# Eleven dense products of a relational graph layer: eight block products against Strassen's seven

## The chip, the cores and the metric

The kernel runs on one core of one Trainium2 chip. The metric is the device time of one execution in microseconds (us), lower being better.

## The reference

The input is `x` (1250 rows of 1024 float32) and 20000 edges, each with a source row, a destination row (the edges are sorted by destination) and one of eight types. What is computed:

```python
h = relu(layernorm(x))                       # 1250 x 1024
u = h @ root + bias
for r in range(8):                           # edge types
    sums = segment_sum(h[src] * (type == r), dst)
    cnt  = segment_sum(type == r, dst)
    u += (sums / maximum(cnt, 1)) @ weight[r]
z = concat([u, h]) @ w_gate + b_gate         # w_gate is 2048 x 1024
out = x + tanh(u) * z + h * (1 - z)
```

So there are eleven dense products of 1250x1024 by 1024x1024: eight with `weight[r]`, one with `root`, and two with the halves of `w_gate`. All of them are float32.

## The kernel before, in words

The rows are cut into ten blocks of 128 (the last has 98). The kernel multiplies first and gathers afterwards: it computes `y[r] = h @ weight[r]` for all rows and writes it to DRAM, and an edge then adds one row of `y[type]`, scaled by 1/count, to its destination row.

**The products.** `transposed` (L102, L104) turns a row block into eight 128x128 blocks that are the stationary operand. `product` (L111) runs, for each of the eight pieces of the inner dimension and each half of the 1024 columns, one 128x128 by 128x512 matmul; in the trace each is two MATMUL instructions. The weights are loaded by `load_w` (L92) on SyncE's queue, one matrix ahead. `step(s, d)` does matrix `s` for block `d`: for the eight typed weights ScalarE copies the two PSUM banks out (L174) and writes `y` (L175), for `root` VectorE adds them to `u` (L179), for the lower half of `w_gate` it adds the bias and stores `z` (L183) over the transposed `h`, in the tile `hz`.

**The slots.** Beside the first two matrices, `slots(c0)` takes eight chunks of 128 edges at a time (`CG = 8`) and works out with one-hot comparisons on VectorE and small bf16 matmuls on TensorE the rank of every edge among those of its destination. An indirect DMA from GpSimd (L347) scatters each edge's row number into `table`. There are 26 slots for each destination for types 0 to 4, and 20 for types 5 to 7.

**The edges.** Slots are gathered in two groups: group 0 (types 0 to 4) beside matrices 5 to 7, group 1 (types 5 to 7) beside `root` and the lower half of `w_gate`. For each slot and row block, `add_slot` issues an indirect DMA on GpSimd that brings 128 rows of `y` into the tile `got` (L418; five buffers), and VectorE does `u = got * w + u` (L422). That makes 10 x 26 + 10 x 20 = 460 gathers. The ten blocks of `u` stay in the on-chip memory. A rare path for more slots stands between the groups under a condition and is not taken with these inputs.

**The end.** `finish(d)` transposes `u`, multiplies it by the upper half of `w_gate`, and works out the result on VectorE and GpSimd (L507 to L515).

The order of instructions on each engine is fixed ahead of the run by a planner: it goes through the program with its own durations and takes on each engine, among the instructions that are ready, the one that comes first in the program. A tile's buffer is handed on only when all who use it are done.

Of the kernel before, what the change touches and what calls it, by code (L numbers as in the profile page):

```python
# [18 lines left out]
def tile_rgcn_highway(  # L19
# [22 lines left out]

    nc = tc.nc
# [5 lines left out]
    NH = D // 512  # L49
    ND = -(-N // P)  # L50
    NCH = -(-E // P)
# [8 lines left out]
    CG = 8  # L60
# [9 lines left out]
    wpool = ctx.enter_context(tc.tile_pool(name="wpool", bufs=2 * KC))  # L70
    rows = ctx.enter_context(tc.tile_pool(name="rows", bufs=2))
# [3 lines left out]
    h_dram = dram.tile([N, D], F32, name="h_dram")  # L75
    keys_dram = dram.tile([NCH * P], I32, name="keys_dram")
# [5 lines left out]
    def ps_tr():  # L82
        return psum.tile([P, 4, P], F32, name="ps_tr", bufs=2)

    def ps_mm():
        return psum.tile([P, 512], F32, name="ps_mm", bufs=4)

    def load_w(w):
        tiles = []
        for k in range(KC):  # L90
            t = wpool.tile([P, D], F32, name="w_t")
            nc.sync.dma_start(t, w[k * P:(k + 1) * P, :])  # L92
            tiles.append(t)
        return tiles

    def transposed(to, of, n):

        for g in range(KC // 4):
            p = ps_tr()
            for i in range(4):  # L100
                k = 4 * g + i
                nc.tensor.transpose(p[:, i, :n], of[:n, k * P:(k + 1) * P], ident[:n, :n])  # L102
            copy = nc.vector.tensor_copy if g % 2 else nc.scalar.copy
            copy(to[:, 4 * g:4 * g + 4, :n], p[:, :, :n])  # L104

    def product(aT, n, w):

        banks = [ps_mm() for _ in range(NH)]
        for k in range(KC):
            for j in range(NH):  # L110
                nc.tensor.matmul(banks[j][:n], aT[:, k, :n], w[k][:, j * 512:(j + 1) * 512],  # L111
                                 start=(k == 0), stop=(k == KC - 1))
        return banks
# [5 lines left out]
    bias_bc = const.tile([P, D], F32, name="bias_bc")  # L119
    bgate_bc = const.tile([P, D], F32, name="bgate_bc")  # L120
# [4 lines left out]
    first = const.tile([P, NCH], F32, name="first")  # L125
    count = const.tile([P, R * ND], F32, name="count")
    drc = const.tile([P, R + G, ND], F32, name="drc")
    runs = const.tile([P, NHI], F32, name="runs")

    hz = [keep.tile([P, D], F32, name=f"hz{d}") for d in range(ND)]  # L130

    def hT(d):
        return hz[d].rearrange("p (k f) -> p k f", k=KC)


    w_t = None
    for d in range(ND):
        n = nrows(d)
        xt = rows.tile([P, D], F32, name="xt")
        nc.sync.dma_start(xt[:n], x[d * P:d * P + n, :])  # L140
        if d == 0:
            w_t = load_w(weight[0])
        st = rows.tile([P, NH, 6], F32, name="st")
        for j in range(NH):
            nc.vector.bn_stats(st[:n, j, :], xt[:n, j * 512:(j + 1) * 512])  # L145
        mv = rows.tile([P, 2], F32, name="mv")
        nc.vector.bn_aggr(mv[:n], st[:n].rearrange("p a b -> p (a b)"))
        sd = rows.tile([P, 1], F32, name="sd")
        nc.scalar.activation(sd[:n], mv[:n, 1:2], AF.Sqrt, bias=eps[:n])
        rs = rows.tile([P, 1], F32, name="rs")  # L150
        nc.vector.reciprocal(rs[:n], sd[:n])
        nc.vector.tensor_scalar(xt[:n], xt[:n], mv[:n, 0:1], 0.0, op0=OP.subtract, op1=OP.max)
        nc.scalar.activation(xt[:n], xt[:n], AF.Copy, scale=rs[:n])  # L153
        nc.sync.dma_start(h_dram[d * P:d * P + n, :], xt[:n])
        transposed(hT(d), xt, n)


    mats = [weight[r] for r in range(R)] + [root, w_gate[D:, :]]
    cur = {"w": w_t, "next": None}

    def step(s, d):

        n = nrows(d)
        if d == 0:
            if s:
                cur["w"] = cur["next"]
            cur["next"] = load_w(mats[s + 1] if s + 1 < len(mats) else w_gate[:D, :])
        banks = product(hT(d), n, cur["w"])
        if s < R:
            g = max(i for i in range(G) if R0[i] <= s)  # L170
            o = (s - R0[g]) * N + d * P
            t = rows.tile([P, D], F32, name="yt", bufs=3)
            for j, b in enumerate(banks):
                nc.scalar.copy(t[:n, j * 512:(j + 1) * 512], b[:n])  # L174
            nc.scalar.dma_start(y[g][o:o + n, :], t[:n])  # L175
        elif s == R:
            for j, b in enumerate(banks):
                c = slice(j * 512, (j + 1) * 512)
                nc.vector.tensor_add(u_acc[d][:n, c], u_acc[d][:n, c], b[:n])  # L179
        else:  # L180
            for j, b in enumerate(banks):
                c = slice(j * 512, (j + 1) * 512)
                nc.vector.tensor_add(hz[d][:n, c], b[:n], bgate_bc[:n, c])  # L183

    steps = iter([(s, d) for s in range(len(mats)) for d in range(ND)])


    with ExitStack() as early:
        ix1 = early.enter_context(tc.tile_pool(name="ix1", bufs=1))
        ix = early.enter_context(tc.tile_pool(name="ix", bufs=2))  # L190

        far = ix1.tile([P, sum(n_slots) // P], I32, name="far")
        nc.gpsimd.memset(far, FAR)
        nc.scalar.dma_start(table.rearrange("(p f) o -> p (f o)", p=P), far)


        C2 = NCH - P
        ed = {}
        for name, of, pad in (("dst", dst, 3 * KEYS), ("typ", etype, R), ("src", src, 0)):
            t = ix1.tile([P, 2, P], I32, name=f"e_{name}")  # L200
            nc.gpsimd.memset(t[:, 1, :], pad)
            nc.scalar.dma_start(t[:, 0, :], of[:P * P].rearrange("(c p) -> c p", p=P))
            nc.scalar.dma_start(t[:C2 - 1, 1, :],
                                of[P * P:(NCH - 1) * P].rearrange("(c p) -> c p", p=P))
            nc.scalar.dma_start(t[C2 - 1:C2, 1, :EL], of[None, (NCH - 1) * P:])
            ed[name] = t
        nc.scalar.dma_start(bias_bc, bias[None, :].to_broadcast([P, D]))
        nc.scalar.dma_start(bgate_bc, b_gate[None, :].to_broadcast([P, D]))

        f = {}  # L210
        for name in ("dst", "typ", "src"):
            f[name] = ix1.tile([P, 2, P], F32, name=f"f_{name}")
            nc.vector.tensor_copy(f[name], ed[name])
        blk_i = ix1.tile([P, 2, P], I32, name="blk_i")
        nc.vector.tensor_single_scalar(blk_i, ed["dst"], 7, op=OP.arith_shift_right)
        blk = ix1.tile([P, 2, P], F32, name="blk")
        nc.vector.tensor_copy(blk, blk_i)
        late = ix1.tile([P, 2, P], F32, name="late")
        nc.vector.tensor_single_scalar(late, f["typ"], float(R0[1]), op=OP.is_ge)
        key = ix1.tile([P, 2, P], F32, name="key")  # L220
# [297 lines left out]
    for d in range(ND):  # L518
        finish(d)
# [24 lines left out]
```

## Time and profile before

| | |
|---|---|
| median of three runs | 1635.64 us (1634.98 to 1637.37) |
| profiled execution, its own time | 1634.76 us |
| its span, first to last instruction | 1632.8 us |
| granted TensorE clock, mean | 0.985 |
| TensorE busy (matmuls) | 1570.1 us, 96% |
| VectorE busy | 903.3 us, 55% |
| GpSimd busy | 753.6 us, 46% |
| ScalarE busy | 130.7 us, 8% |

The profile is one execution; its own time is 1.96 us more than its span, and 0.9 us under the median of the three runs. Busy shares are means over stages with different work: 20 steps with the slots, 30 steps with products alone, 30 with group 0 of the edges, 20 with group 1, and the ten finishing steps. They are read stage by stage.

### The profile page before, as it was taken

The numbers are of one execution on the slowest core, as the hardware profiler recorded it, in microseconds if no ns is written. First come the engines' busy times: TensorE is split into PE (matmuls) and PEld (weight loads), VectorE is DVE, ScalarE is ACT, GpSimd is POOL, SyncE is SP. The second block draws the span as 40 slices with busy tenths as digits, with TensorE's granted clock in tenths as the row PEclk, the third lists the DMA queues.
The fourth block names the chain that finished last, engine by engine and source line by source line (L and its number), as shares of the span: only waits on it lengthen the run. The fifth ranks groups of instructions, "written<-read, shape, count | busy, mean of one in ns | idle before, by whom it ended". The sixth has DMA issues, their size and how long they took to land.

```text
span 1632.8 us, 13043 instructions
## 1 busy us (share of the span) xinstructions
PE 1570.1 (96%) x4158; PEld 697.1 (43%) x4158; DVE 903.3 (55%) x1513; ACT 130.7 (8%) x212; POOL 753.6 (46%) x655
## 2 busy tenths in 40 slices
PE   5998869999999999999999999999999999999798
PEld 2544334444444444444444444444444444444343
DVE  3587656631000000000688688688878989998743
ACT  1310000000000000000000000000000000001000
POOL 0047645552000000000677577677757777777821
PEclk8999989999999999999999999999999999999899
DMA  8625743253013003003555755755654353422620
GB/s 300 251 75 88 120 114 78 48 100 84 39 51 126 39 39 139 38 35 121 177 167 165 266 166 167 267 172 172 199 167 125 109 181 105 132 75 70 219 72 36
DMA packets 108218, 207.89 MB, mean 127 GB/s; under 512 B 57063, under 2 KB 57816, under 8 KB 108146
## 3 DMA queue, kind: packets, MB, share of 16 engines
q0 software_dynamic: 70528, 82.19, 17.0%
q1 hardware_dynamic: 20896, 66.86, 12.9%
q10 hardware_dynamic: 16722, 57.98, 11.4%
q8 instruction: 32, 0.52, 0.2%
q14 instruction: 40, 0.33, 0.1%
HBM read 308.83 MB, written 51.60 MB: 221 GB/s over the span
## 4 chain that ended last, share of the span: by engine, by line
PE 85%; DMA 6%; DVE 3%; issue 3%; POOL 2%; ACT 1%; POOLq 0%; ACTq 0%; DVEq 0%; SPq 0%
PE ps_mm L111 84%; DMA table<-row_col,at_i 2%; DMA k_bc<-keys_dram 2%; POOL table L347 1%; DVE junk L332 1%; POOL got L508 1%; PE ps_tr L102 1%; DVE u L422 1%; DMA w_t<-in_L_gnn_weight_dram 0%; DMA table<-far 0%; DMA e_src<-in_src_dram 0%; ACT xt L104 0%; DVE hz L515 0%; DMA xt<-in_x_dram 0%; DMA keys_dram<-key_i 0%
## 5 line engine op out<-in xcount | busy, mean ns | idle before, releaser
L111 PE MATMUL ps_mm<-w_t,hz 128*128 128x512 f32 (+1 forms) x3200 | 1398.6, 598 | 0.9 <-ACT hz L104 0.9
L111 PEld LDWEIGHTS ps_mm<-w_t,hz 128*128 128x128 f32 (+1 forms) x3200 | 600.4, 189 | 756.5 <-issue 747.9
L418 POOL DMA_INDIRECT got<-y,idx x460 | 525.8, 1143 | 596.0 <-DMA y<-yt 398.7
L422 DVE SCALAR_TENSOR_TENSOR u<-got,w,u 128x1024 f32<-128x1024 f32 (+1 forms) x450 | 587.3, 1306 | 95.2 <-DMA got<-y,idx 83.3
L347 POOL DMA_INDIRECT table<-row_col,at_i x157 | 164.9, 1050 | 206.0 <-DVE junk L332 100.5
L422 DVE SCALAR_TENSOR_TENSOR u<-got,w,bias_bc 128x1024 f32<-128x1024 f32 (+1 forms) x10 | 12.8, 1284 | 400.6 <-DMA got<-y,idx 400.3
L174 ACT COPY yt<-ps_mm 128x512 f32<-128x512 f32 (+1 forms) x160 | 93.5, 585 | 1015.5 <-PE ps_mm L111 989.7
L111 PE MATMUL ps_mm<-w_t,xt 128*128 128x512 f32 (+1 forms) x320 | 144.2, 609 | 12.4 <-ACT xt L104 9.6
L111 PEld LDWEIGHTS ps_mm<-w_t,xt 128*128 128x128 f32 (+1 forms) x320 | 60.5, 192 | 90.1 <-issue 74.3
L332 DVE SCALAR_TENSOR_TENSOR junk<-k_bc,key_col,before 128x128 f32<-128x128 int32 x157 | 49.5, 345 | 30.3 <-DMA k_bc<-keys_dram 30.3
L300 DVE TENSOR_TENSOR seen<-seen,ps_n 128x20 f32<-128x20 f32 x157 | 26.5, 169 | 34.5 <-PE ps_n L297 32.2
L509 POOL TENSOR_TENSOR u<-u,yt 128x1024 f32<-128x1024 f32 (+1 forms) x10 | 25.8, 2583 | 40.7 <-ACT u L507 40.7
L513 DVE TENSOR_TENSOR hz<-hz,ps_mm 128x512 f32<-128x512 f32 (+1 forms) x20 | 13.6, 684 | 55.5 <-PE ps_mm L111 55.5
L104 ACT COPY xt<-ps_tr 128x512 f32<-128x512 f32 (+1 forms) x10 | 5.8, 575 | 409.4 <-PE ps_tr L102 357.0
L508 POOL TENSOR_TENSOR got<-got,yt 128x1024 f32<-128x1024 f32 (+1 forms) x10 | 31.0, 3110 | 14.0 <-DMA yt<-h_dram 9.5
L321 PE MATMUL ps_q<-s_b,to_lo 128*128 128x40 bf16 x157 | 7.3, 182 | 24.2 <-DVE s_b L312 24.2
L102 PE MATMUL ps_tr<-ident,xt 128*128 128x128 f32 (+1 forms) x80 | 12.1, 302 | 17.3 <-ACT xt L153 17.3
L515 DVE TENSOR_TENSOR hz<-hz,got 128x1024 f32<-128x1024 f32 (+1 forms) x10 | 25.0, 2501 | 2.3 <-POOL got L508 2.2
L283 DVE TENSOR_TENSOR is_lo<-lo_col,io 128x1024 bf16<-128x1024 f32 (+1 forms) x20 | 23.9, 1196 | 0.0
L321 PEld LDWEIGHTS <-to_lo 128*128 128x128 bf16 x157 | 6.4, 98 | 37.4 <-DVE s_b L312 33.1
L315 DVE TENSOR_SCALAR l_bc<-k_bc 128x1024 int32<-128x1024 int32 (+1 forms) x20 | 13.8, 692 | 15.0 <-DMA k_bc<-keys_dram 15.0
L145 DVE BATCH_NORM_STATS2 st<-xt 128x6 f32<-128x512 f32 (+1 forms) x20 | 12.8, 683 | 14.7 <-DMA xt<-in_x_dram 14.7
(112 smaller groups left out, 300.8 us busy)
## 6 DMA issues: line engine op xcount, KB each, us to landing
y<-yt ACTq DMA_DIRECT2D x72, 512.0 KB
w_t<-in_L_gnn_weight_dram SPq DMA_DIRECT2D x64, 512.0 KB
k_bc<-keys_dram ACTq DMA_DIRECT2D x19, 512.0 KB
w_t<-in_L_gnn_w_gate_dram SPq DMA_DIRECT2D x16, 512.0 KB
got<-y,idx POOLq DMA_INDIRECT x460, 3.7
xt<-in_x_dram SPq DMA_DIRECT2D x9, 512.0 KB
h_dram<-xt SPq DMA_DIRECT2D x9, 512.0 KB
yt<-h_dram SPq DMA_DIRECT2D x9, 512.0 KB
```

The costliest lines, as they stand in the source:

```text
L102: nc.tensor.transpose(p[:, i, :n], of[:n, k * P:(k + 1) * P], ident[:n, :n])
L111: nc.tensor.matmul(banks[j][:n], aT[:, k, :n], w[k][:, j * 512:(j + 1) * 512], start=(k == 0), stop=(k == KC - 1))
L174: nc.scalar.copy(t[:n, j * 512:(j + 1) * 512], b[:n])
L283: nc.vector.tensor_tensor(t[:, :m, :], of[:, c0:c1, None].to_broadcast([P, m, width]), io[:, None, :width].to_broadcast([P, m, width]), op ...
L300: nc.vector.tensor_add(seen[:, c + 1, :], seen[:, c, :], p[:, i * NHI:(i + 1) * NHI])
L332: nc.vector.scalar_tensor_tensor(junk, k_bc[:, i, :], key_col[:, c:c + 1], before, op0=OP.is_equal, op1=OP.mult, accum_out=rank[:, c:c + 1])
L347: ins = nc.gpsimd.indirect_dma_start(out=table[:, :], out_offset=bass.IndirectOffsetOnAxis(ap=at_i[:n, i:i + 1], axis=0), in_=row_col[:n, ...
L418: nc.gpsimd.indirect_dma_start(out=t[:n], out_offset=None, in_=y[g][:, :], in_offset=bass.IndirectOffsetOnAxis(ap=idx[:n, d, k:k + 1], axi ...
L422: nc.vector.scalar_tensor_tensor(u_acc[d][:n], t[:n], w[:n, d, k:k + 1], (bias_bc if fresh else u_acc[d])[:n], op0=OP.mult, op1=OP.add)
L508: nc.gpsimd.tensor_add(xt[:n], xt[:n], ht[:n])
L509: nc.gpsimd.tensor_sub(u[:n], u[:n], ht[:n])
L515: nc.vector.tensor_add(z[:n], z[:n], xt[:n])
```

## The change

The row blocks are taken in pairs (block `i` and block `i + 5`), so a product of a pair is a 2x2 block product: two row blocks by two halves of the inner dimension, times four 512x512 quarters of the weights. Strassen's scheme (in Winograd's form) makes it with seven products of quarters in place of eight. `right` works out the combined quarters of a weight matrix, with four subtractions of 128x2048 on VectorE; `left` works out the combined stationary blocks of a pair, with four operations of 128x512. `product` runs the seven products in PSUM banks from one ring of seven, with four copies on ScalarE and three additions on VectorE.

`u` lies in DRAM: it is filled with the bias at the start, and `edges` loads a block, adds its slots and stores it, in each of the two groups. `upool` holds two blocks of `u`; `got` has four buffers. `h @ root` goes to DRAM and is added to `u` at the end of group 1's block. `slots` takes four chunks at a time (`CG = 4`) and is called after every second product of quarters; the edges are spread over the products in the same way. The pools of the edges are closed before the last stage opens its own pool, where one tile `ht` takes first `h` and then `x`, for one row block after the other.

The core of the diff (all of the functions that the numbers below go by; the conversion of the index columns, which moves into a pool of its own, is left out):

```diff
-    CG = 8
+    CG = 4
+    A11, A12, A22, S1, S2, S3, S4 = range(7)
+    A21 = S3
...
+    def bank():
+        return psum.tile([P, 512], F32, name="ps", bufs=7)
     def load_w(w):
+        q = {}
+        for i, j in ((0, 0), (0, 1), (1, 1), (1, 0)):
+            t = wpool.tile([P, KQ, Q], F32, name="wq", bufs=8)
+            nc.sync.dma_start(t, w[i * Q:(i + 1) * Q, j * Q:(j + 1) * Q].rearrange("(k p) n -> p k n", p=P))
...
+    def right(q):
+        t1, t2, t4 = [wpool.tile([P, KQ, Q], F32, name="wt", bufs=3) for _ in range(3)]
+        nc.vector.tensor_sub(t1, q[0, 1], q[0, 0])
+        nc.vector.tensor_sub(t2, q[1, 1], t1)
+        nc.vector.tensor_sub(q[0, 1], q[1, 1], q[0, 1])
+        nc.vector.tensor_sub(t4, q[1, 0], t2)
+        return {A11: q[0, 0], A12: q[1, 0], S4: q[1, 1], A22: t4, S1: t1, S2: t2, S3: q[0, 1]}
...
+    def left(aop):
+        nc.vector.tensor_add(aop[:, S1], aop[:, A21], aop[:, A22])
+        nc.vector.tensor_sub(aop[:, S2], aop[:, S1], aop[:, A11])
+        nc.vector.tensor_sub(aop[:, S3], aop[:, A11], aop[:, A21])
+        nc.vector.tensor_sub(aop[:, S4], aop[:, A12], aop[:, S2])
+    def product(aop, w, t, to=None, between=lambda: None):
...
+        def add(b, i, fresh):
+            for k in range(KQ):
+                nc.tensor.matmul(b, aop[:, i, k, :], w[i][:, k, :], start=(fresh and k == 0),
+                                 stop=(k == KQ - 1), skip_group_check=True)
+            between()
+        b, c = bank(), bank()
+        add(b, A11, True)
+        nc.scalar.copy(p1, b)
+        add(c, S1, True)
+        nc.scalar.copy(p5, c)
+        add(b, S2, False)
+        nc.scalar.copy(u2, b)
+        a = bank()
+        add(a, A12, True)
+        nc.vector.tensor_add(to[0][0], p1, a)
+        add(b, S3, False)
+        nc.vector.tensor_add(to[1][1], p5, b)
+        add(c, S4, False)
+        nc.vector.tensor_add(to[0][1], u2, c)
+        add(b, A22, False)
+        nc.scalar.copy(to[1][0], b)
...
+    nc.scalar.dma_start(u_dram, bias[None, :].to_broadcast([N, D]))
...
+        def edges(g):
+            idx, w = slot_tiles(g, table[o:o + n_slots[g], :], SLOTS[g])
+            for i in range(ND):
+                d = i // 2 + (i % 2) * NP
+                u = upool.tile([P, D], F32, name="u")
+                nc.sync.dma_start(u[:n], u_dram[at, :])
+                for k in range(SLOTS[g]):
+                    add_slot(u, g, d, k, idx, w)
+                    yield
+                if g == G - 1:
+                    t = gpool.tile([P, D], F32, name="got")
+                    nc.sync.dma_start(t[:n], hr_dram[at, :])
+                    nc.vector.tensor_add(u[:n], u[:n], t[:n])
+                nc.sync.dma_start(u_dram[at, :], u[:n])
...
+    last = ctx.enter_context(tc.tile_pool(name="last", bufs=1))
+    for i in range(NP):
+        op = last.tile([P, 7, KQ, P], F32, name="u_op")
+        for part in range(2):
+            u = last.tile([P, D], F32, name="u2", bufs=2)
+            nc.sync.dma_start(u[:n], u_dram[at, :])
+            transposed(op, part, u, n)
+            nc.scalar.activation(u[:n], u[:n], AF.Tanh)
+        left(op)
+        product(op, w_u, t)
+        for part in range(2):
+            ht = last.tile([P, D], F32, name="ht")
+            nc.sync.dma_start(ht[:n], h_dram[at, :])
+            nc.gpsimd.tensor_sub(u[:n], u[:n], ht[:n])
+            nc.vector.tensor_add(z[:n], z[:n], bgate_bc[:n])
+            nc.vector.tensor_add(z[:n], z[:n], c[:n])
+            nc.vector.tensor_mul(z[:n], z[:n], u[:n])
+            nc.vector.tensor_add(z[:n], z[:n], ht[:n])
+            nc.sync.dma_start(ht[:n], x[at, :])
+            nc.vector.tensor_add(z[:n], z[:n], ht[:n])
+            nc.scalar.dma_start(out[at, :], z[:n])
```

## The prediction

> **What bounds the kernel now.** I read the page's slices first, then a table by stage, the stages' waits, and the chain.
>
> ```profile
> PE   5998869999999999999999999999999999999798
> DVE  3587656631000000000688688688878989998743
> POOL 0047645552000000000677577677757777777821
> ```
>
> TensorE looks like the only limit. From the twentieth slice on, however, VectorE and GpSimd are nearly as full. The same by stage (engines in the order PE, PEld, DVE, ACT, POOL), the bounds put where matrix 4 ends, where group 0 of the edges runs, where group 1 runs, and behind it:
>
> ```profile
> 0.00:773.00 773.00, 730.00 (x2157) 327.35 (x2158) 221.98 (x955) 77.85 (x130) 171.26 (x175) 0.98 0.35 98
> 785.00:1193.00 408.00, 408.00 (x952) 178.29 (x951) 334.07 (x260) 35.10 (x60) 287.70 (x257) 1.00 0.59 195
> 1201.00:1520.00 319.00, 315.09 (x754) 139.12 (x753) 290.30 (x249) 7.55 (x9) 242.24 (x201) 1.00 0.38 113
> 1520.00:1633.00 113.00, 96.98 (x252) 43.57 (x250) 52.77 (x40) 9.16 (x12) 45.09 (x16) 0.95 0.30 108
> ```
>
> Group 0's gathers take 408 us beside three matrices, and VectorE is busy for 334 of them. Group 1 is later than TensorE: its last addition ends at 1522, when the finishing products have run since 1461 and TensorE has had to wait for `u`. So a second chain, gather by gather, is as long as TensorE's from 785 to 1522. Its price per slot:
>
> ```profile
> L418 POOL DMA_INDIRECT got<-y,idx x460 | 525.8, 1143 | 596.0 <-DMA y<-yt 398.7
> L422 DVE SCALAR_TENSOR_TENSOR u<-got,w,u 128x1024 f32<-128x1024 f32 (+1 forms) x450 | 587.3, 1306 | 95.2 <-DMA got<-y,idx 83.3
> ```
>
> In quiet parts the additions follow each other every 1.32 us (1.285 and the step to the next), and so do the gathers on GpSimd (1.02 busy and 0.30 between). The rest is waiting for gathered rows; VectorE's waits in 785 to 1195 (the 398.2 among them is the wait ahead of the first gather, which leaves 65.5), and the gathers' landing times:
>
> ```profile
> DVE u L422 <- DMA got<-y,idx: 463.7, 64, 398.2
> ```
>
> ```profile
> DMA to landing us min/median/max: 2.1/4.1/12.2
> ```
>
> In group 1 it is 19.8 us. TensorE's price and a quiet load of 512 KB come from the chain in order of time:
>
> ```profile
> 365.95 1094.38 PE ps_mm L111 x2550
> 1514.44 3.19 DMA got<-in_x_dram
> ```
>
> **TensorE: what is removed.** 1094.38/2550 is 0.4292 us for a MATMUL. A matrix is 160 matmuls, 320 MATMUL: 137.3 us; seven products of quarters, four matmuls each, for five pairs are 280: 120.2 us. A product of quarters is 8 x 0.4292 = 3.43 us. Eleven matrices save 11 x 17.1 = 189 us of TensorE's own work. If TensorE stayed the bound, the span would be 1632.8 - 189 = 1444. The Trainium skill, Perfetto Trace Analysis, section Identifying the Most-Contended Engine, says that the engine with the highest occupancy is the one to optimize first, which is TensorE with 96%: by that rule the sum ends near 1444. I go by the rows of the two edge stages, where another chain is as long.
>
> **Stage 1, to the end of matrix 4.** Before: 773, of which 5 x 137.3 = 686.5 is products and 86.5 start, transposes, slot matmuls and waits. After: 601 + 86.5, plus two additions. (a) The start: filling `u` with the bias writes 5.1 MB, where the two bias loads wrote 1.0; at the 300 GB/s of the first slice that is 14 us, on ScalarE's queue ahead of the index loads, and `right` has 9 us before the third product of the first step. Between 0 and 30; I take 10, since part lies beside the load of the weights. (b) The slots: the rows of L283 to L343 sum to 231 us of VectorE. With four chunks a group there are 20 more groups, each repeating some 20 small operations with about 0.1 us that does not shrink: 40. With 36 additions of 0.684 (25) and two `right` (18) that is 314 us in the twelve steps that hold the slots, where TensorE has 12 x 24 + 23 = 311. VectorE, 62% busy there before, has no reserve left, and TensorE waits for each group's one-hots. Between 0 and 60; I take 20. Stage 1: 717. The first addition of group 0 follows 13 us later, as now (773 to 785.6): 730.
>
> **Group 0.** Three matrices are 360 us on TensorE (412 before). VectorE's work, by rows of this tile:
>
> ```profile
> L513 DVE TENSOR_TENSOR hz<-hz,ps_mm x20: 673/686/689, 1474.6 to 1625.6; 128x512 f32<-128x512 f32 x18, 98x512 f32<-98x512 f32 x2
> L514 DVE TENSOR_TENSOR hz<-hz,u x10: 1210/1224/3351, 1517.9 to 1626.4; 128x1024 f32<-128x1024 f32 x9, 98x1024 f32<-98x1024 f32 x1
> ```
>
> An addition from PSUM is 0.684. A subtraction of 128x2048 is in no row: at most two of 1.224 (2.45), and by the slope from 260 elements (0.429) to 1024 (1.224) 2.29; I take 2.3. 45 additions are 31 us, three `right` of four 28. So VectorE has at least 260 x 1.32 + 59 = 402 us: more than TensorE, whatever the gathers do. To the measured 408 I add: the fifth buffer of `got`, and the 59 us. Four buffers cover a landing of 4 x 1.32 - 1.29 - 0.30 = 3.7 us, five one of 5.0, and the median is 4.1; the 65.5 us of waiting grow by between nothing and their double: I take a third, 22. Of the 59 us, a quarter falls into waits (87 of 430 us): 44. The next load of `u` has the second buffer and is free. Sum 408 + 22 + 44 = 474.
>
> ScalarE, with four copies of 0.585 in 24 us, hides. TensorE is held back: the seventh product reuses the bank that the addition after the fifth must have read, so it leads VectorE by less than one product, and the matrices after the edges cannot run ahead.
>
> **Between the groups.** SyncE, in order, stores the last `u` behind the last addition, passes the condition and loads the index tile, which now has one buffer (before, both indices were loaded early): store and load issue 0.33 each, landing 3.2 or more beside 4 MB of weights, a gather 1.0 + 2.1. Between 8 (now: 1193 to 1201) and 30; I take 14.
>
> **Group 1.** Before 319, with 40 additions (27 us). After: 30 additions (20.5), ten of 1.22 for `h @ root`, two `right` (18.4): 51, so 24 more, three quarters of it 18; a third more waiting 7. Sum 344, against TensorE's 240.
>
> **The end.** Before, 113 us lie behind the last gathered addition, since several finishing products had run beside the edges. After, the last stage's tiles take the place of the edges' tiles and start after them. In each pair `ht` and `u2` have no spare buffer, so from the end of the sixth product a chain runs through to the next pair's second product: addition 0.69, three operations of 1.22, load of x 3.5 (3.19 + 0.33 issue), 1.22, load of h 3.5, GpSimd's subtraction 2.35 (its median at L509), 1.22, load of the next u 3.5, transposes 0.9, copy 0.6, `left`'s first 0.7: 21.8. With five products of 3.43 the period is 39, where TensorE has 24. First pair to the end of its sixth product: release, load, transposes, copy, 6 x 3.43: 28. Four periods: 156. Last pair: 22 to the end of its chain, 4 for the output as now: 26. Sum 210; between 165 (the planner finds work for the waits) and 260 (slower operations beside GpSimd, as L514's longest of 3.35). The granted clock was 0.93 in 100 to 200, with 11 us idle, and I add nothing for it. The Trainium skill, TensorE: Matmul & The Clock Gate, section What's actually happening, says that after an idle window of about 3.4 us the clock is halved and comes back after a busy one: by that, an estimate, four waits add 4 x 1.7 = 7 us.
>
> **Sum.** 730 + 474 + 14 + 344 + 210 = 1772; the profiled execution before took 1634.76 with a span of 1632.8, 2 more, and its time stands 0.9 under the median. Forecast 1774, 139 over the median.
>
> **Rivals.** (A) The last stage runs beside group 1: four of its five pairs hide, 1774 - 156 = 1618, faster. It decides if at least 139 of the 156 hide. For it: TensorE has 100 us free there, and before the stages did overlap. Against: the code closes the edges' pools before `last` opens. (B) Loads and stores of `u` in DRAM are ordered one after the other: at 18 inner changes of block VectorE waits for a store (0.33 + 2.88, the store of `h` in the chain) and a load (3.5): 18 x 6.7 = 121, 1895. For it: a load behind a store in one queue; against: they are different rows and there are two buffers. (C) The gathers land in time: VectorE alone sets the stages, 402 + 14 + 315 in place of 832: 1673. Against: weight loads and writes of `y` come as often as before, and the waits stood beside them. (D) TensorE stays the bound, 1446 with the 2 us: excluded by 402 against 360, unless additions cost less than any row shows.
>
> **How the numbers follow.** Forecast 0.78, A 0.06, B 0.07, C 0.07, D 0.02. Unknowns of the forecast: start and slots -30 to +60, buffers and quarters +-40, the end -45 to +50; together some +-90. Range 1680 to 1865, which leaves out A, B, D and most of C. 0.2% is about what a measurement can tell from no change. Faster are A and D, and nearly all of A: 0.07; same 0.01; slower 0.92.
>
> **What would show it.** Right: TensorE near 100% only up to the fifth matrix, busy about 75% beside group 0 and 70% beside group 1, waiting for VectorE's PSUM additions; VectorE above 85% there; `got` waiting on buffers; in the end a period near 39 us with VectorE and GpSimd waiting for loads of `ht`. Wrong: edge stages of 360 and 240 us, or products of the last stage beside gathers.

## The result, and the profile after

The changed kernel takes 1886.01 us (median of four runs, 1884.87 to 1897.71) where the kernel before takes 1635.31 (four runs): the ratio is 1.155, with an interval of 1.150 to 1.160. Two runs on record, one of the kernel before (2092 us) and one of the first version under the last heading of the experiments (3280 us), fell into a slow state and are left out of the medians. The profiled execution took 1884.95 us with a span of 1883.1; its stages are set against the prediction's terms here (us of span; before in the last column):

| stage | predicted | after | before |
|---|---|---|---|
| start to the end of matrix 4 | 717 | 761.8 | 773.1 |
| to the first gathered addition | 13 | 10.2 | 12.5 |
| group 0 (260 gathers) | 474 | 484.3 | 407.2 |
| between the groups | 14 | 14.1 | 8.7 |
| group 1 (200 gathers) | 344 | 363.9 | 321.0 |
| behind the last gathered addition | 210 | 248.8 | 110.4 |
| span | 1772 | 1883.1 | 1632.8 |

So the loss of 250 us is 77 in group 0, 43 in group 1, 138 in the end and 5 between the groups, less 14 up to the first addition. The miss of 111 us is 45 in the first row, 39 in the last, 20 in group 1 and 10 in group 0, less 3.

The slices of the page of the changed kernel (47 us each), with the granted clock:

```profile
PE   0498989899999999999898998999897000066664
DVE  3877867673210202577788778768888778653332
POOL 0034454353000000466676767656676777410010
PEclk9999999899999999999999999999998555577777
```

The reader sees three things that the old page had not: an empty first slice on TensorE, four empty slices ahead of the last stage while VectorE and GpSimd still work on group 1, and a last stage at six tenths with the clock at seven. The same as a table by stage (PE, PEld, DVE, ACT, POOL, granted clock, DMA share, GB/s; lines between are left out):

```profile
0.00:89.00 89.00, 21.01 (x87) 16.54 (x87) 50.65 (x97) 20.29 (x31) 2.15 (x15) 1.00 0.76 273
...
772.00:1257.00 485.00, 443.29 (x986) 192.38 (x985) 388.55 (x326) 40.61 (x70) 327.93 (x257) 0.95 0.56 186
...
1270.00:1635.00 365.00, 166.36 (x362) 71.63 (x360) 296.81 (x239) 14.65 (x25) 252.25 (x197) 0.72 0.44 138
1635.00:1883.00 248.00, 143.45 (x360) 69.13 (x360) 91.34 (x96) 29.14 (x41) 24.73 (x12) 0.78 0.27 87
```

No engine is full in any of them. TensorE did get shorter: matrices 3 and 4, with nothing beside them, take 119.7 us from first to last matmul, where they took 136.9; that is the promised eighth. Behind matrix 4 it buys nothing, since TensorE is through with group 1's matrices at 1451 and then stands. From the waits of the whole run:

```profile
PE ps L120 <- DMA u<-u_dram: 262.6, 10, 190.6
...
POOL u L603 <- DMA ht<-h_dram: 183.5, 9, 34.9
```

190.6 us of it are one wait: the last stage's first transposes wait for a `u` that group 1 has not finished. The price of a slot, from the costliest groups:

```profile
L479 POOL DMA_INDIRECT got<-y,idx x460 | 587.0, 1276 | 586.8 <-DMA y<-pair 311.2
...
L483 DVE SCALAR_TENSOR_TENSOR u<-got,w,u 128x1024 f32<-128x1024 f32 (+1 forms) x460 | 590.7, 1284 | 164.5 <-DMA got<-y,idx 155.3
```

The addition costs what it did; the gather's issue on GpSimd grew from 1143 to 1276 ns, and VectorE's idle time ahead of the additions from 95 to 165 us. The waits in 772 to 1257, group 0:

```profile
DVE u L483 <- DMA got<-y,idx: 91.8, 75, 7.7
POOL got L479 <- DVE u L483: 85.5, 68, 4.3
...
PE ps L140 <- DVE pair L155: 41.7, 13, 7.3
```

VectorE waits for rows and GpSimd waits for a free `got`: these two make a ring, in which each waits for the other in turn. TensorE, which waits for VectorE's additions from PSUM, hangs on it. Of the 91.8 us, 7.7 are the wait ahead of the first gather, so 84.1 and 85.5 us are to be set against 65.5 and 36.5 before. The second of these is this line of the kernel before (785 to 1193):

```profile
POOL got L418 <- DVE u L422: 36.5, 29, 4.6
```

### The profile page after: what moved, and what is told of

Read it like the earlier page. It is cut to its first block, busy times and chain, and to the rows that moved or that the text cites. A ratio compares the mean times of both kernels' runs of the same rounds, so it can differ in the third digit from the quotient of the medians.

```text
span 1883.1 us, 13218 instructions
## 1 busy us (share of the span) xinstructions
PE 1433.9 (76%) x3718; PEld 643.6 (34%) x3718; DVE 1145.3 (61%) x2136; ACT 166.7 (9%) x272; POOL 780.6 (41%) x648
## 5 line engine op out<-in xcount | busy, mean ns | idle before, releaser
L479 POOL DMA_INDIRECT got<-y,idx x460 | 587.0, 1276 | 586.8 <-DMA y<-pair 311.2
L140 PE MATMUL ps<-wq,h_op 128*128 128x512 f32 x1600 | 711.8, 595 | 0.0
L140 PE MATMUL ps<-wt,h_op 128*128 128x512 f32 x1200 | 577.3, 631 | 57.1 <-DVE pair L155 45.5
L140 PEld LDWEIGHTS ps<-wq,h_op 128*128 128x128 f32 x1600 | 301.2, 191 | 364.0 <-issue 363.9
L140 PEld LDWEIGHTS ps<-wt,h_op 128*128 128x128 f32 x1200 | 237.7, 202 | 354.8 <-issue 281.1
L153 DVE TENSOR_TENSOR pair<-pair,ps 128x512 f32<-128x512 f32 x50 | 34.3, 686 | 202.3 <-PE ps L140 201.2
L159 ACT COPY pair<-ps 128x512 f32<-128x512 f32 x50 | 29.3, 586 | 750.5 <-PE ps L140 692.5
L140 PE MATMUL ps<-wq,u_op 128*128 128x512 f32 x160 | 76.6, 635 | 0.0
L155 DVE TENSOR_TENSOR pair<-pair,ps 128x512 f32<-128x512 f32 x50 | 34.3, 685 | 57.0 <-PE ps L140 56.7
L157 DVE TENSOR_TENSOR pair<-pair,ps 128x512 f32<-128x512 f32 x50 | 34.3, 685 | 51.4 <-PE ps L140 51.3
L140 PE MATMUL ps<-wt,u_op 128*128 128x512 f32 x120 | 53.2, 593 | 0.8 <-DVE u_op L126 0.8
L150 ACT COPY pair<-ps 128x512 f32<-128x512 f32 x55 | 32.2, 586 | 181.6 <-PE ps L140 181.6
L148 ACT COPY pair<-ps 128x512 f32<-128x512 f32 x55 | 32.2, 586 | 179.3 <-PE ps L140 171.6
L146 ACT COPY pair<-ps 128x512 f32<-128x512 f32 x55 | 32.2, 586 | 164.3 <-PE ps L140 153.8
L140 PEld LDWEIGHTS ps<-wq,u_op 128*128 128x128 f32 x160 | 33.0, 210 | 39.7 <-issue 39.7
```

The costliest lines, as they stand in the source:

```text
L140: nc.tensor.matmul(b, aop[:, i, k, :], w[i][:, k, :], start=(fresh and k == 0), stop=(k == KQ - 1), skip_group_check=True)
L146: nc.scalar.copy(p1, b)
L148: nc.scalar.copy(p5, c)
L150: nc.scalar.copy(u2, b)
L153: nc.vector.tensor_add(to[0][0], p1, a)
L155: nc.vector.tensor_add(to[1][1], p5, b)
```

## The experiments

The theory was that the gathers' ring and the last stage's loads set the time, not TensorE; the rivals put it on the seven products themselves, or on `u` in DRAM. The kernel before took 1668 us on the chip of four of the runs (the fill, the end, both together, and the first version under the last heading) and 1633 on that of the others, so those four are read by stages or against 1668. The changed kernel itself, run again on the second chip, gave 1887.72 us with stages within 3 us of the table. On the first of the two chips it was not run; stages that an edit left alone came out within 3 us of the table there too, but for group 1 (up to 372.6) and one matrix of the run with both edits (10 us). All runs but those under the last heading are single ones. Four runs of the changed kernel spread over 13 us, so a difference of about ten in a whole time is not clear of noise.

> The changed kernel itself, on the chip of the three runs below, so that their stages can be set beside it: 1885 as before, within 10 us, with 762 us to the end of matrix 4, 484 and 364 us for the two groups and 249 behind them.

### The start: fill and order

The timeline of the changed kernel's start (us, duration, engine; "ACTq" is ScalarE's sequencer):

```profile
2.13 13.68 ACTq L258 DMA_DIRECT2D e_dst<-in_dst_dram  x1
...
18.27 1.28 ACT L189 ACT_TABLE_LOAD   x1 [18.27 <-issue]
...
34.46 1.15 ACT L193 ACTIVATE pair<-pair,rs 128x1024 f32<-128x1024 f32 x1 [13.04 <-DMA u_dram<-in_L_gnn_bias_dram]
```

An index load behind the 5000 KB fill holds ScalarE's sequencer for 13.68 us, so the first normalization begins at 18; and another 13 us pass until the fill has landed. The first product starts at 88.9. First, the fill alone is taken out:

```diff
-    nc.scalar.dma_start(u_dram, bias[None, :].to_broadcast([N, D]))
-                nc.sync.dma_start(u[:n], u_dram[at, :])
+                nc.sync.dma_start(u[:n], u_dram[at, :] if g else bias[None, :].to_broadcast([n, D]))
```

> The start. Group 0 loads each block of u straight from the bias row, so the 5 MB fill of u in DRAM is gone and all else stays. Theory (the fill makes the start late: ScalarE's issue of the next index load took 13.7 us behind it and ScalarE then waited 13.0 us more for it): the first product starts 25 to 35 us earlier than 88.9, the time is 1850 to 1860 instead of 1885. Rival (the first product stands behind the transposes of all ten blocks in TensorE's order, and x, h and the weights need that long anyway): under 10 us, 1875 or more.

Measured: 1864.47 us, 21.5 less than the change's median. The first product starts at 62.8 and matrix 4 ends at 735.7, both 26 earlier. The later stages came out 2 us longer here and there, so the time missed its expectation by 5.

What was left of the start was tried on top of that: each pair's step of the first matrix is written directly behind the pair's transposes, the first `right` moves ahead of the other pairs, and the slots begin one matrix later.

```diff
         left(h_op[i])
         if i == 0:
             w_raw[0] = load_w(mats[0])
+            w_t[0] = right(w_raw[0])
+        step(0, i)
-    w_t = {0: right(w_raw[0])}
-    steps = iter([(s, i) for s in range(len(mats) - 1) for i in range(NP)])
+    steps = iter([(s, i) for s in range(1, len(mats) - 1) for i in range(NP)])
```

> The kernel without the fill of u, in which the step of the first matrix for a pair is written directly behind the pair's transposes (so it comes before the other pairs in the program), and the slots begin with the second matrix. Without the fill alone: first product at 62.8 us, matrix 4 ends at 735.7, 1864.5 in all. Theory (the rest of the start is the order: all ten transposes ahead of the first product on TensorE, and right's subtractions ahead of the other pairs on VectorE): the first product at 25 to 40, matrix 4 ending at 705 to 725, the time 1835 to 1855. Rival (the start waits for the loads of x and of the weights, whatever the order, and the slots set the time of the matrices beside them): matrix 4 ending at 728 or later.

Measured: 1827.16 us, below the 1835 to 1855 expected. The timeline of TensorE in this kernel:

```profile
9.04 3.65 PE L120 MATMUL ps<-ident,pair 128*128 128x128 f32 x16 [9.04 <-ACT pair L220]
12.48 4.55 PE L140 MATMUL ps<-wq,h_op 128*128 128x512 f32 x8
16.86 3.60 PE L140 MATMUL ps<-wt,h_op 128*128 128x512 f32 x8
```

Products run from 12.5 on, and matrix 4 ends at 700.5. So the start's excess was the fill (26 us) and the order (35, the move of the slots included): with ten transposes first on TensorE, the first product waited for the last block's load and normalization. Loads of `x` or of weights did not force it.

### The end: the tiles of the last stage

The chain of waits of the changed kernel, in order of time, over one period (start, us, what):

```profile
1716.15 0.70 DVE pair L157
...
1720.71 4.44 DMA ht<-in_x_dram
1725.24 1.24 DVE h_op L609
1726.50 4.92 DMA ht<-h_dram
1731.55 2.35 POOL u L603
1733.92 1.24 DVE h_op L606
1735.17 3.38 DMA u<-u_dram
...
1738.69 1.94 PE ps L120 x8
1740.63 22.43 PE ps L140 x48
1763.15 0.70 DVE pair L157
```

From addition to addition it is 47.0 us, through three loads that take each other's place in `ht` and `u2`. The experiment gives `u`, `h` and `x` tiles of their own, in weight tiles that are free by then:

```diff
+    scratch = [wpool.tile([P, KQ, Q], F32, name="wq", bufs=8) for _ in range(4)]
-            u = last.tile([P, D], F32, name="u2", bufs=2)
+            u = row_of(scratch[i % 2], part)
-            ht = last.tile([P, D], F32, name="ht")
+            ht, xt = row_of(scratch[2], part), row_of(scratch[3], part)
+            nc.sync.dma_start(xt[:n], x[at, :])
```

> The end. In the last stage the loads of h, x and u get buffers of their own for both halves of a pair (and u for two pairs), in the four weight tiles that are free there; the arithmetic stays. Theory (the single buffers of ht and u2 chain three loads into each pair's period of 46.4 us): the period falls to 26 to 31 us, the stage behind the last gathered addition from 249 to 160 to 185, the time to 1800 to 1820. Rival (TensorE's halved clock sets the period): the period stays above 40, the time above 1865.

Measured: 1825.71 us, 60 less; behind the last gathered addition 179.4 us in place of 248.8, as expected. From first product to first product of the pairs it is 28.0 us once and then 33.8, more than the 26 to 31 of the theory. The time missed its range by 6, because group 1, which the edit leaves alone, took 372.6 here. Both edits in one kernel:

> Both edits together, no fill and buffers of their own in the last stage. If the start and the end are separate terms of a sum, their gains add within 8 us; theory 1770 to 1795. If the edge stages take back what the start gives (their chain has its own pace, so it should not), the sum is short by more than 10 us.

Measured: 1802.36 us, 84 less than the change's median, where the two alone gave 21.5 and 60.3: they add up, a little above the range expected. Neither touches what happens in the groups (482.4 and 368.1).

### The seven products, or the frame

First, the frame without the scheme: eight products per matrix, accumulated in PSUM, four copies on ScalarE, no combined quarters or blocks, and everything else as changed.

```diff
...
+        for r, (l0, l1) in enumerate(((A11, A12), (A21, A22))):
+            banks = [bank(), bank()]
+            for j in range(2):
+                add(banks[j], l0, w[0, j], True)
+                add(banks[j], l1, w[1, j], False)
+            for j in range(2):
+                nc.scalar.copy(to[r][j], banks[j])
```

> The other part of the change alone: pairs, u in DRAM, four buffers and the last stage stay, but every product is made of eight products of quarters that add up in PSUM, with no sums of quarters on either side and four copies on ScalarE; VectorE has no work for the products. TensorE gets 17 us more a matrix, 189 in all. Theory (the gathers' chain and the frame set the end, the saved seventh counts in matrices 0 to 4 only, and VectorE's work for it costs in the edge stages): matrices 2 to 4 take 137 us each instead of 120 to 130, group 0 takes 425 to 450 us instead of 484, group 1 320 to 345 instead of 364, and the time stays within 40 us of the changed kernel's, 1845 to 1905. Rival 1 (TensorE is the bound): 1885 + 189, 2040 or more. Rival 2 (the seven products themselves are the loss, not the frame): 1720 or less.

Measured: 1898.72 us, in the range. Matrix 4 ends at 829.6, 66 us later than in the run of the changed kernel on the same chip, yet the whole is only 11 slower than with seven products. Group 0 took 474.2 and group 1 348.4, so taking all of the scheme's work off VectorE gave 12 and 15 us against that run, where the theory had 35 to 60 and 19 to 44: the expectation was missed in both. The end gave more: 214.4 us behind the last gathered addition against 247.5. The three loads follow each other there as before, but the period is 38 to 40 us, because VectorE's chain goes on after four products of quarters behind the transposes and not after six:

```profile
1735.71 14.43 PE ps L134 x32
1750.16 0.59 ACT pair L144
```

So the seven products gain 66 us up to matrix 4 and give back 12, 15 and 33 in the groups and the end. The loss of 250 us against the kernel before is thus not in their work: the frame alone, with eight products and still four buffers, takes as long.

Next, the subtractions of `right` alone are left out, with the raw quarters in their place:

```diff
-        nc.vector.tensor_sub(t1, q[0, 1], q[0, 0])
...
+        return {A11: q[0, 0], A12: q[1, 0], S4: q[1, 1], A22: q[1, 0], S1: q[0, 1], S2: q[1, 1], S3: q[0, 1]}
```

> Leaves out the four subtractions of 128x2048 for each weight matrix; raw quarters are taken in place of the combined ones, so what is multiplied is not the reference's. Theory (VectorE's and GpSimd's work per slot sets the edge stages; a gather issued beside two of these subtractions took 2.8 us instead of 1.0): 20 subtractions of 2.3 us fall in the edge stages, group 0 gets 20 to 35 us shorter and group 1 10 to 25, the time 1825 to 1855. Rival (the gathers' landings set the pace, VectorE has room): under 12 us in the two groups together.

Measured: 1884.12 us; group 0 took 486.4, no less than the 485.9 before the edit on that chip, and group 1 355.7 in place of 363.6. The two together gave 7 us, as the rival had it. VectorE's busy time within group 0 fell by 27 us (388.6 to 361.5), and the waits (770 to 1262) took all of it:

```profile
DVE u L478 <- DMA got<-y,idx: 131.9, 90, 14.9
```

Of the 131.9 us, 14.9 are the wait ahead of the first gather; the rest is 117 against 84.1. With four buffers, the subtractions were not on the path in group 0.

Then the reverse, whether the gathers set the stage at all: every second slot is left out.

```diff
-                    add_slot(u, g, d, k, idx, w)
+                    if k % 2 == 0:
+                        add_slot(u, g, d, k, idx, w)
```

> Leaves out every second slot of the edges, its gather and its addition, so half the edges are missing from the result. Theory (the chain of gathers sets both edge stages): they fall to TensorE's own pace, group 0 from 484 to 360 to 385 us, group 1 from 364 to 240 to 265, the time to 1650 to 1680. Rival (TensorE's clock or its waits for PSUM banks set them): both stay within 30 us of 484 and 364.

Measured: 1682.95 us, 3 over the range. The 130 gathers of group 0 took 247.6 us, 1.90 each where it was 1.86, and the 100 of group 1 213.6. In between GpSimd waited for the slot weights of group 1, whose first addition came at 1179, while TensorE was full:

```profile
POOL got L479 <- DVE w L468: 155.6, 1, 155.6
```

```profile
1022.00:1179.00 157.00, 157.00 (x367) 69.74 (x366) 33.51 (x35) 15.80 (x27) 3.61 (x4) 1.00 0.33 110
```

TensorE's matrices ran to 1447, and the last stage's transposes followed at once, without the wait of 190.6 us. So with half the gathers TensorE's matrices are the longer chain, and with all of them the gathers are. Beside the gathers TensorE still waits for VectorE (218 us busy of 248 in group 0), so its own pace, as the theory had it, it reached only without them.

### The buffers of `got`

The size that sets the ring was changed alone: three buffers, and five (five need the room of the rare path, which is left out).

```diff
-        gpool = edges_part.enter_context(tc.tile_pool(name="gpool", bufs=4))
+        gpool = edges_part.enter_context(tc.tile_pool(name="gpool", bufs=3))
```

> The tile got has three buffers in place of four. New theory (after the run without the subtractions, in which VectorE lost 30 us of work and group 0 stayed at 486: the pace is set by the ring of got, a buffer being taken from the issue of its gather to the end of its addition, some 6.5 us): group 0 rises from 485 to 560 to 640 us, group 1 from 364 to 430 to 500, the time by 140 to 290. Rival (VectorE's sum of work sets the pace, as the prediction's arithmetic had it): under 20 us in the two groups together.

> The tile got has five buffers, as in the kernel before; the room comes from a scratch tile of the slot weights and from the rare path, which these inputs do not take and which is left out. New theory (the ring): group 0 falls from 485 to 435 to 460 us, group 1 from 364 to 335 to 355, the time to 1825 to 1865. Rival (VectorE's sum of work): both groups within 8 us of 485 and 364.

Measured: 2039.09 us with three (groups of 574.6 and 431.5), 1826.64 with five (459.6 and 339.1), both as the theory had it. Waits of VectorE for rows and of GpSimd for a free buffer in group 0, with three and then with five:

```profile
DVE u L483 <- DMA got<-y,idx: 186.6, 141, 7.4
POOL got L479 <- DVE u L483: 171.1, 119, 4.8
```

```profile
DVE u L483 <- DMA got<-y,idx: 68.3, 53, 7.5
...
POOL got L479 <- DVE u L483: 60.0, 48, 4.3
```

171, 85.5 and 60 us with three, four and five: each buffer that is missing is paid for at this place. Eight buffers find room when the scheme's tiles are gone, so eight products were run with eight:

> The kernel of eight products in the changed frame, with eight buffers of got in the room that the combined quarters had. It had 474 and 348 us for the groups with four buffers, and the kernel before has 407 and 321 with five. New theory (the ring, and not u in DRAM): group 0 falls to 395 to 425, group 1 to 300 to 325. Rival (loading and storing u at each of the twenty changes of block): both stay above 455 and 340.

Measured: 1767.15 us, groups of 372.8 and 291.1, below the expected ranges and shorter than before the change, with `u` in DRAM all the while. TensorE is full beside group 0, as it was before the change (with eight products and four buffers it was busy for 462 of 475 us). From 845 to 1260:

```profile
845.00:1260.00 415.00, 415.00 (x969) 184.27 (x968) 335.35 (x267) 35.69 (x61) 280.01 (x258) 1.00 0.63 215
```

The additions stand nearly back to back (39 us of gaps in 373). Not all of the gain is kept: the pause between the groups grew to 45 us (17.5 with four buffers), since SyncE stores the last `u` and loads the indices of group 1 only after a weight load that it issued from 1234 to 1245.

Two runs at five buffers, the number of the kernel before, show what the scheme costs there: eight products, and seven without the subtractions.

> Eight products per matrix, no combined quarters or blocks, in the changed kernel's frame, with five buffers of got (with four, group 0 took 474.2 us and group 1 348.4). The seven products with five buffers took 459.6 and 339.1, with VectorE 385 us busy and 68 us waiting for gathers in group 0; the kernel before, with five buffers and u on the chip, took 407.2, with 334 busy and 65.5 waiting. Theory (with five buffers the scheme's additions and subtractions, 51 us, lie on the path of group 0): 405 to 430 us in group 0 and 305 to 330 in group 1. Rival (u in DRAM and the weights' quarters make the gathers land later, whatever VectorE does): 445 to 465 in group 0.

> The kernel with five buffers and without the rare path, in which the four subtractions of right are left out too, the products using the raw quarters in their places (27 us less of VectorE in group 0, 18 in group 1); the additions from PSUM stay. Beside it: 459.6 and 339.1 us for the groups with the subtractions. With four buffers taking them out changed group 0 by nothing. Theory (at five buffers VectorE's work is on the path): 430 to 442 in group 0, 318 to 330 in group 1. Rival (the rate is the landing's, as with four buffers): 455 to 462 in group 0.

Measured: 1819.80 and 1806.55 us. Group 0 took 426.3 with eight products and 440.6 without the subtractions, group 1 320.8 and 329.3, against 459.6 and 339.1: all four as the theory said. So at five buffers 19 of the 27 us of subtractions lie on the path of group 0, and at four none. The eight products at five buffers, 842 to 1268:

```profile
842.00:1268.00 426.00, 426.00 (x994) 189.05 (x993) 333.73 (x260) 35.69 (x61) 289.81 (x257) 1.00 0.61 206
```

VectorE is 334 us busy, as before the change.

### Where seven products pay

In the kernel before, only matrices 2 to 4 stand alone on TensorE, with neither slots nor edges beside them. The scheme was put there alone, over pairs of blocks, and everything else was left as it was:

```diff
+    with tc.tile_pool(name="seven", bufs=1) as seven:
+        for s in range(2, R0[1]):
...
-    while True:
-        s, d = next(steps)
-        step(s, d)
```

> One part of the change alone, in the kernel before: seven products of quarters only for matrices 2, 3 and 4, which have no slots and no edges beside them; u stays on the chip, five buffers of got, the last stage as before. Theory (TensorE is the bound only where nothing else runs): three matrices of 120 in place of 137.3, and everything behind them 51 us earlier less a few us at the borders: 1582 to 1597. Rival (seven products cost TensorE what they save, by a lower clock or waits for banks): 1625 or more.

Measured: 1636.68 us (median of three) against 1667.0 (median of six) on the same chip, a ratio of 0.984 (0.978 to 0.989), so -30 and not -51; the range of 1582 to 1597 had been worked out from the 1635 of another chip. Matrices 3 and 4 took 119.7 us, matrix 2 145.5, with one wait at the border:

```profile
PE ps_mm L419 <- DVE sl L410: 21.3, 1, 21.3
```

The tiles of `seven` stand where the slots' tiles were, and the first combination waited for the last scatter. So the second version leaves the first pair of matrix 2 to the old eight products, which need no new tile:

> Seven products of quarters in the kernel before, for matrices 2 to 4 but for the first pair of matrix 2, whose two blocks are made the old way. In the first try TensorE stood 21 us at the border, where the combined quarters wait for the room of the slots' pools; the two old products (27 us) lie over that. Theory: 14 products of a pair of 24.0 us in place of 27.5, 48 us less and at most 6 us at the border: 40 to 49 us faster than the kernel before on the same chip. Rival (the edges' chain behind it gives part of it back, or seven products cost TensorE waits): under 30 us.

Measured in five runs: 1587.70 us (1584.24 to 1591.48) against 1632.55 beside it, a ratio of 0.9725 (0.9705 to 0.9744), 44.9 us less, within the expected range and better than both kernels. The stretch that the scheme now has to itself:

```profile
390.00:726.00 336.00, 336.00 (x784) 148.77 (x783) 81.52 (x127) 32.73 (x56) 0.00 (x0) 1.00 0.21 76
```

TensorE is full and VectorE, with all of the scheme's additions, works 82 of 336 us. Groups 0 and 1 take 409.1 and 319.5 us behind it, against 407.2 and 321.0 in the kernel before.

## Why the prediction was wrong, point by point

The direction held, and so did the two chains that the prediction named: the gathers and the last stage's loads bound the kernel, and behind matrix 4 the eighth saved on TensorE fell into waits. What failed are terms of the sum, the start and the period of the end above all. In group 0 the mechanism was half right: the prediction added VectorE's work to the old time, while with four buffers the ring of `got` set the pace and the subtractions, 27 us of that work, cost nothing. The forecast of 1774 lies 112 under the time, and the range ended 21 below it. The steps, by size:

- **The start (term a).** It was given 10 us, at most 30. The fill alone cost 26 (its run), and another 35 came from a place that the prediction had not costed at all: the order, all ten blocks' transposes ahead of the first product (its run). With both gone matrix 4 ends at 700.5, which is 13 us over 601 + 86.5; the 20 us put down for the slots (term b) were thus nearly right. The prediction priced the fill by its bytes, 14 us; ScalarE's wait for it ended at 34 us, and what it did was hold ScalarE's sequencer, with the normalizations queued behind it.
- **The end.** The chain was the one predicted, and so was the count of periods, but each was 47.0 us and not 39. Of the 8, 2.6 are loads (4.44 and 4.92, and the step to the next operation, in place of 3.5 each); 2.1 are the first product of the next pair, 3.4 us that the prediction let run beside the chain and that stood behind the transposes of both halves, less the copy and `left`, which it hid in turn; 2.9 are TensorE being slower after its wait (transposes 1.94 for 0.9, and 22.43 us for 48 MATMUL, 20.6 at 0.4292). The first pair took 35.5 and not 28. For the slower TensorE the prediction had taken nothing, from a row in which the clock stayed at 0.93 over small gaps; here the granted clock of the stage is 0.78, and the rows give 2.9 us a period, so 11 to 12 us over four. The rule of the Trainium skill (TensorE: Matmul & The Clock Gate, What's actually happening), weighed and not taken, would have given an estimate of 7; these rows side with the rule and lie above its estimate.
- **Group 0.** The sum of 474 was 10 short, but two of its terms were not what they seemed. The fifth buffer was put at 22 us and VectorE's 59 us of work at 44, added up. The runs: with five buffers the scheme costs 33 us (459.6 to 426.3), with four 10 to 12 (474.2 left); the buffer costs 25 with the scheme and 48 without. Alone they are 48 and 33, together 58 and not 81, so part of one falls into the waits of the other. The rest, 19 us against the 407.2 of before, is the frame, put at nothing: about 5 at the changes of block, where `u` comes from DRAM, and the remainder in gaps between additions. The gathers landed 4.91 us after their issue on the mean there, and 4.49 before the change, but no run separates the cause. That the sum came within 10 us is in part luck: VectorE's work was put too high for four buffers, the buffer and the frame too low.
- **Group 1.** Buffer and scheme were put at 25 us over 319; together they cost 43 (363.9 to 320.8). The buffer was the mis-sized term: 7 predicted, 25 measured with the scheme in place (363.9 to 339.1). The frame added nothing there.
- **Between the groups and matrix times.** 14 against 14.1, 120.2 against 119.7, the subtraction of 128x2048 at 2.29 against 2.3, the PSUM addition 0.685 against 0.684: these prices were right.
- **What the profile was to show.** TensorE near 100% only up to the fifth matrix, `got` waiting for buffers, and a period of waits on `ht`: seen. VectorE above 85%: no, 80 and 81%. TensorE 75 and 70% busy: no, 91 and 46%. The statement that matrices after the edges cannot run ahead was wrong: TensorE did run ahead and had finished group 1's matrices at 1451, because VectorE's fixed order has the PSUM additions well before the gathered additions that they were written beside (the last of them starts at 1447, when 92 of group 1's 200 gathered additions have started). It cost nothing, since the last stage could not start in any case.
- **The rivals.** A (the end hidden) is refuted by the 190.6 us wait; it would have needed the pools to be open side by side. B asked for 121 us at 18 changes of block; their gaps sum to 28.7 us, 7.3 of which are also there before. C needed landings in time; VectorE waited 84 us for them within group 0 alone. D, TensorE as the bound at 1446, comes only where the gathers are cut: half of them gave 1683, with TensorE's matrices as the longer chain. The sum of 1444 that the prediction drew from the rule of the busiest engine (the Trainium skill, Perfetto Trace Analysis, Identifying the Most-Contended Engine) did not come: 1886. The rule says which engine to optimize first and not what that is worth, and for TensorE the section has headroom judged by other measures than the matmul busy share, the 96% here. Read over 390 to 726 alone, where TensorE is full and VectorE is busy for 82 of 336 us, work on the busiest engine gained 44.9 us.

All remedies together would come, as an estimate from the single runs, to 1886 - 21.5 (fill) - 37.3 (order, against the run without the fill) - 60.3 (end) - 59.4 (five buffers, with the rare path out; 10 of it lies between the groups), about 1708: still slower than before. The combination was not run.

## What to carry to other kernels

Price a saving on the fullest engine only in stages where that engine is the last to arrive, and apply it only there: the change lost 250 us over the whole kernel, and its scheme, put on three matrices of eleven with nothing else changed, won 45. The room that a change takes is a cost like its instructions: look up which ring of buffers pays for it, and what one place of it is worth, since one buffer less cost 25 to 48 us in group 0, where all of the scheme's work on VectorE cost 10 to 33. A large transfer at the start is priced by what is queued behind its issue, and the order of the first instructions on the bounding engine by when the last of their inputs arrives.

## What the runs showed of the hardware

- A DMA issue on ScalarE behind a transfer of 5000 KB took 13.68 us of its sequencer; without the fill the same load's issue took 0.40.
- A gather's issue on GpSimd took 0.99 us with VectorE idle (28 cases) and 2.80 beside two of the four subtractions of 128x2048 (10 cases, on L109 and L110); begun during an addition from PSUM it stayed at 0.99 (25 cases). Over the whole kernel the issues took 587 us against 526. The subtractions are only part of that: within group 0 the issues took 334 us in the changed kernel, 320 without the subtractions, 296 with eight products and 291 before the change.
- With eight buffers the gathers of group 0 took 1.43 us a slot, against 1.82 with four, both with eight products in the changed frame. The 1.57 of the kernel before, with five buffers, is thus not the least that the transfer of the rows allows, and more buffers there would be worth a trial, which was not made.
- The granted clock fell to half in the four slices in which TensorE stood ahead of the last stage, and after each wait of that stage the first matmuls were slower: 0.24 us for a transpose (eight in 1.94). In the first 89 us the record shows a clock of 1.00, though eight transposes took 1.97 us there too.
